# Two-layer graph transformer convolution on Trainium2: another order of the steps in a round

## The chip, the cores and the metric

The kernel runs on one core of one Trainium2 chip. The metric is the time of the program on the device in microseconds (us); lower is better. The kernel before was timed in three runs, with a median of 2658.26 us (2657.74 to 2663.06).

## The reference

The graph has 6250 nodes of 128 features and 106250 edges (self loops among them), sorted by destination. An edge's 96 attributes are 32 cosines of a time difference and 64 given numbers. Two transformer convolutions with two heads run one after the other, with a batch norm and a relu between them; a residual and a layer norm follow.

```python
def _transformer_conv(h, edge_attr, src, dst, Wq, bq, Wk, bk, Wv, bv, We, Ws, bs):
    q, k, v = ...                                   # (n, H, C) each, C = 64
    e = (edge_attr @ We).reshape(-1, H, C)
    kj = k[src] + e
    alpha = jnp.einsum('ehc,ehc->eh', q[dst], kj) / jnp.sqrt(C)
    amax = segment_max(alpha, dst, num_segments=n)
    ex = jnp.exp(alpha - amax[dst])
    den = segment_sum(ex, dst, num_segments=n)
    a = ex / den[dst]
    out = segment_sum((v[src] + e) * a[:, :, None], dst, num_segments=n)
    return out.reshape(n, H * C) + h @ Ws + bs
...
rel_t_enc = jnp.cos((last_update[src] - t)[:, None] * time_w[None, :] + time_b)
edge_attr = jnp.concatenate([rel_t_enc, msg], axis=-1)
h = relu(batch_norm(_transformer_conv(x, edge_attr, src, dst, ...)))
h = _transformer_conv(h, edge_attr, src, dst, ...)
x = layernorm(x + h)
```

## The kernel before

The edges are cut into 104 chunks of 1024 (eight tiles of 128). `conv(c, ...)` runs once for each convolution, c = 0 and c = 1, and its main loop (from L1203) does one round for each chunk. A round k works on several chunks at different stages: it fetches one some rounds ahead, turns k + 1, scores k, sums k − 1, joins k − 2 and finishes k − 3. The order is written out by hand: the loop calls the steps below one after the other, and every engine runs its instructions in the order in which they were called. SP's queue carries most loads and stores, GpSimd's (POOL) the gathers, ScalarE's (ACT) a few others.

The steps, with their lines:

- fetch (from L900): SP loads a chunk's query tables (`ftab`), in c = 1 also its attribute features and residual rows.
- gather (L942): eight indirect transfers on POOL bring the source rows of a chunk into one of seven ring slots (`fring`), a tile each. Through `bring(rows, behind)` a gather can be made to wait for a TensorE step, so that gathers keep TensorE's pace.
- encode (L975 to L988) and sine (L994), c = 0 only: VectorE (DVE) reduces the angles of the cosine, `farg`, and ACT applies the sine. For chunks 43 to 84 encode runs three rounds ahead of the chunk, for the others two; in the former the sine is done for two chunks at once. place (L997) stores the attributes, ea_d.
- feature transposes (`turn_rows`, L1015, tile `fpx`) with ACT's copy to `fft` (L1019), and in c = 0 attribute transposes (`turn_terms`, L1027, `fpe`) with the copy to `fet` (L1028) and a store by SP to et_d. Each of the two is done in two halves of four tiles.
- score (L1058, `fps`): the attention scores. lowest (L1066, L1068): DVE takes their minimum, `fm`. weigh (L1073): ACT's exponential, `fs`.
- weights' transposes (`turn_weights`, L1082, `fppt`) and ACT's copy `fpt` (L1083).
- sums (`gather_sums`, L1105, `fpa`): weighted sums of the gathered rows and attributes. They need fpt.
- divide (L1114 to L1121): DVE divides by the weights' sum (`finv`, `fa`) and makes a selection matrix (`fsel`).
- joins (`finish_turn`, L1136): two transposing matmuls through `fsel` into the same PSUM buffer, and DVE's copy `fat` (L1138).
- product (L1144/1145 in c = 0, L1150/1151 in c = 1): the projection of `fat`, again into that buffer. complete (L1166 in c = 0, from L1173 in c = 1) reads it and adds the skip or residual (`fres`); store (L1183 to L1186) ends c = 1.
- mark (L927 to L930), c = 0: which node of the group an edge belongs to.
- tables: in most rounds one piece of other work is pulled from a list (L635 to L643 the tables of later chunks, `fpg`; L1398 and what follows for the batch norm).

All transposes and tables share four PSUM buffers. The scores have one buffer in c = 0 and two in c = 1. `fpa` has two: the sums of a chunk take the buffer of the chunk two before, once complete has read it.

## Time and profile before

| | |
|---|---|
| median of three runs | 2658.26 us |
| the profiled execution's own time | 2659.45 us |
| its span in the profile | 2657.7 us |
| TensorE (PE) busy | 1857.7 us, 70% |
| GpSimd (POOL) busy | 1583.8 us, 60% |
| VectorE (DVE) busy | 1139.7 us, 43% |
| ScalarE (ACT) busy | 965.5 us, 36% |
| DMA engines busy, mean | queue of SP and ACT loads 36.8%, of the gathers 17.1% |

The profile is of one execution. Its span runs from the first to the last instruction; 1.75 us of the time lie around it. A row of the timeline gives the start, the duration, engine, line and operation, written and read tiles, and in brackets how long the engine stood idle before it and what ended that. "issue" means that the profile shows nothing that the engine waited for, "remote" that the releaser is not known. The ends of matmuls are modelled.

### The profile page before, as it was taken

The page shows a single profiled execution, that of the slowest core. Times are in us where ns is not written, and L with a number is a line of the kernel's source. Part 1 is how long each engine was busy: PE and PEld are TensorE (multiplying, and loading weights), DVE is VectorE, ACT ScalarE, POOL GpSimd, SP SyncE. Part 2 cuts the span into 40 slices and gives each one's busy share as a digit, 9 for nine tenths or more (in the row PEclk, how much of TensorE's full clock was granted, in tenths as well). Part 3 has the DMA queues.
Part 4 walks back from the last instruction along what each step waited for, and adds up shares of the span by engine and source line. Part 5 has one row for each costly group of instructions (what it writes and reads, how often), then busy time and mean ns, then how long its engine had stood idle before and what let it go on. Part 6 is the DMA issues. An engine that isn't in the chain of part 4 may idle for free.

```text
span 2657.7 us, 43186 instructions
## 1 busy us (share of the span) xinstructions
PE 1857.7 (70%) x13293; PEld 1010.6 (38%) x13293; DVE 1139.7 (43%) x3734; ACT 965.5 (36%) x1838; POOL 1583.8 (60%) x1687
## 2 busy tenths in 40 slices
PE   5476776777777777676776676777776776776676
PEld 3243343444333434343443333333333333333333
DVE  4465556556555555465644322332223322232223
ACT  1355545544344343354552222222222222222222
POOL 5256666666666666666626666666666666666663
PEclk9699988989889888889787888888788878788878
DMA  6366665666566665666647555555646555556452
GB/s 181 98 193 181 175 173 158 175 171 176 154 181 175 177 166 158 183 160 177 164 138 211 155 140 149 167 150 149 171 136 171 144 149 158 158 139 171 136 138 69
DMA packets 426919, 423.56 MB, mean 159 GB/s; under 512 B 297362, under 2 KB 344384, under 8 KB 423352
## 3 DMA queue, kind: packets, MB, share of 16 engines
q1 hardware_dynamic: 353174, 273.15, 36.8%
q0 software_dynamic: 53184, 109.31, 17.1%
q10 hardware_dynamic: 20322, 38.24, 4.0%
q8 instruction: 109, 1.79, 0.3%
q14 instruction: 130, 1.06, 0.1%
HBM read 274.63 MB, written 142.54 MB: 157 GB/s over the span
## 4 chain that ended last, share of the span: by engine, by line
PE 56%; issue 23%; another core or an unknown queue 8%; ACT 5%; DVE 4%; DMA 2%; SPq 1%; POOL 1%; ACTq 0%; DVEq 0%; POOLq 0%
PE fps L1058 15%; PE fpa L1105 14%; PE fpx L1015 8%; PE fpg L635 5%; PE fpe L1027 4%; PE fppt L1082 3%; PE fpa L1136 2%; PE fpa L1144 1%; PE fpa L1150 1%; PE fpa L1151 1%; ACT fft L1019 1%; ACT L994 1%; DVE fa L1117 1%; DMA fring<-hn_d,fsrcs 1%
## 5 line engine op out<-in xcount | busy, mean ns | idle before, releaser
L942 POOL DMA_INDIRECT fring<-xv_d,fsrcs x814 | 772.6, 949 | 523.9 <-issue 173.0
L942 POOL DMA_INDIRECT fring<-hn_d,fsrcs x774 | 736.4, 951 | 436.8 <-issue 166.8
L1083 ACT COPY fpt<-fppt 128x384 f32<-128x384 f32 x208 | 100.0, 481 | 1337.5 <-remote 642.4
L1105 PE MATMUL fpa<-fring,fpt 128*32 128x256 f32 (+1 forms) x4128 | 470.1, 504 | 143.2 <-issue 136.7
L1058 PE MATMUL fps<-fft,ftab 128*32 128x384 f32 (+1 forms) x1774 | 330.8, 564 | 46.7 <-issue 27.7
L1105 PEld LDWEIGHTS fpa<-fring,fpt 128*32 128x32 f32 (+1 forms) x4128 | 155.4, 140 | 463.9 <-issue 370.6
L1066 DVE TENSOR_REDUCE flow<-fps 128x1 f32<-128x384 f32 x207 | 115.4, 558 | 499.6 <-PE fpx L1015 288.7
L1015 PE MATMUL fpx<-fident,fring 128*128 128x128 f32 x1664 | 278.8, 295 | 66.4 <-issue 56.2
L1027 PE MATMUL fpe<-fident,fring 128*112 128x128 f32 x832 | 145.4, 302 | 213.1 <-issue 206.0
L1019 ACT COPY fft<-fpx 128x512 f32<-128x512 f32 x402 | 233.3, 581 | 112.5 <-remote 63.2
L1015 PEld LDWEIGHTS fpx<-fident,fring 128*128 128x128 f32 x1664 | 213.9, 153 | 84.3 <-issue 70.5
L1027 PEld LDWEIGHTS fpe<-fident,fring 128*112 128x112 f32 x832 | 101.6, 145 | 237.2 <-issue 229.0
L1058 PE MATMUL fps<-fxT,ftab 112*32 112x384 f32 (+2 forms) x900 | 177.4, 556 | 14.0 <-issue 13.6
L1114 DVE TENSOR_SCALAR finv<-fpa 128x1 f32<-128x1 f32 x206 | 32.7, 159 | 359.4 <-PE fps L1058 88.2
L1136 PE MATMUL fpa<-fsel,fa 128*128 128x128 f32 x404 | 89.6, 304 | 121.1 <-issue 65.1
L1058 PE MATMUL fps<-fet,ftab 112*32 112x384 f32 (+2 forms) x960 | 159.4, 454 | 8.6 <-issue 8.3
L1058 PEld LDWEIGHTS fps<-fft,ftab 128*32 128x32 f32 x1774 | 99.6, 126 | 142.1 <-issue 90.3
L987 DVE SCALAR_TENSOR_TENSOR farg<-fangles,farg 128x256 f32<-128x256 f32 x312 | 132.3, 424 | 10.7
L1186 DVE TENSOR_SCALAR fout<-fres,fmean,fvar 64x128 f32<-64x128 f32 x104 | 38.2, 367 | 221.6 <-ACT fvar L1184 70.3
L1028 ACT COPY fet<-fpe 112x512 f32<-112x512 f32 x207 | 124.3, 601 | 15.7 <-PE fpa L1105 6.7
L1082 PE MATMUL fppt<-fident,fs 128*128 128x128 f32 x626 | 115.3, 287 | 16.3 <-issue 13.9
L1073 ACT ACTIVATE fs<-fps,fm 128x384 f32<-128x384 f32 x207 | 120.7, 583 | 8.8 <-DVE fm L1068 4.3
(282 smaller groups left out, 2461.1 us busy)
## 6 DMA issues: line engine op xcount, KB each, us to landing
ea_d<-fring SPq DMA_DIRECT2D x104, 448.0 KB
et_d<-fet SPq DMA_DIRECT2D x104, 448.0 KB
fring<-ea_d SPq DMA_DIRECT2D x104, 448.0 KB
fxT<-et_d SPq DMA_DIRECT2D x104, 448.0 KB
tab_d<-fo ACTq DMA_DIRECT2D x26, 1024.0 KB
ftab<-tab_d SPq DMA_DIRECT2D x832, 32.0 KB
fring<-in_edge_attr SPq DMA_DIRECT2D x103, 256.0 KB
fring<-xv_d,fsrcs POOLq DMA_INDIRECT x814
```

Of the source, the lines that this page charges most:

```text
L635: pl.step = nc.tensor.matmul(pg, a, fT, start=True, stop=True)
L942: row = nc.gpsimd.indirect_dma_start(out=f[:, t, :D + 1 - c], out_offset=None, in_=(h_d[:N, :] if k < RAW else hn_d) if c else pl.xv_d, in ...
L987: nc.vector.scalar_tensor_tensor(arg, turn, -part, arg, op0=OP.mult, op1=OP.add)
L1015: last = nc.tensor.transpose(px[:, t * P:(t + 1) * P], s.x[:, u * 4 + t, 1 - c:1 - c + D], ident)
L1019: nc.scalar.copy(s.ft[:, u * GE:(u + 1) * GE], px)
L1027: last = nc.tensor.transpose(pe[:EC, t * P:(t + 1) * P], s.e[:, u * 4 + t], ident)
L1028: copy(s.et[:, u * GE:(u + 1) * GE], pe[:EC])
L1058: steps.append(nc.tensor.matmul(s.ps[r, to:to + n], s.tab[:kd, r, i], (ets if i else fts)[:kd, at:at + n], start=i == 0, stop=i == 1 and t ...
L1073: nc.scalar.activation(s.s[:, :s.ps.shape[1]], s.ps, AF.Exp, bias=s.bias, scale=-1.0)
L1082: last = nc.tensor.transpose(pp[:, t * P:(t + 1) * P], s.s[:, t * P:(t + 1) * P], ident)
L1105: steps.append(nc.tensor.matmul(s.pa[g * GH:(g + of) * GH].rearrange("p (a d) -> p a d", a=2), s.pt[:, (g * n + t) * GH:(g * n + t + of) * ...
L1136: step = nc.tensor.transpose(s.po[:, i], s.a[:, r], s.sel[:, 0])
```

## The change

The calls of a round are put in another order, and the gathers wait for other steps. In c = 0 TensorE's order was: score, product, weights' transposes, joins, half of the features, half of the attributes, the other halves, tables, sums. It is now: features of the next chunk, weights' transposes, score, attributes, product, joins, tables, sums. In c = 1 it is the same without the attributes. ACT's copies follow. On VectorE encode now stands behind divide and ahead of lowest, complete and the joins' copy; it stood behind those three. Where one chunk's sine is done alone, it now comes after the joins, or ahead of the next encode.

The eight gathers of a round waited for: the end of the previous sums, half the scores, weights' transposes, joins, first half and second half of the next chunk's transposes, one third and two thirds of the sums. They now wait for: the end of the previous sums, feature transposes, weights' transposes, half the scores, all scores; then in c = 1 joins, one third and two thirds of the sums, in c = 0 attribute transposes, joins, one third of the sums. On SP's queue the store of et_d and the sending of finished rows move with the steps that issue them.

```diff
--- before.py
+++ after.py
@@ -987,6 +987,9 @@
                 nc.vector.scalar_tensor_tensor(arg, turn, -part, arg, op0=OP.mult, op1=OP.add)
             nc.vector.tensor_scalar(arg, arg, -3 * HALF_PI, HALF_PI, op0=OP.max, op1=OP.min)
 
+        def lone():
+            return len(args) == 2 and not SINGLE <= args[1] < LATE
+
         def sine():
             arg, *of = args
             args.clear()
@@ -1226,11 +1229,12 @@
                     bring(range(T))
                 elif not filling:
                     bring(range(1), ended)
-                half, scored = score(k) if on(k) else (None, None)
-                if k >= -1 and not filling:
-                    bring((1,), half)
-                if on(k - 3) and k <= SWITCH:
-                    product(k - 3)
+                step = turn_rows(k + 1, 0) if on(k + 1) else None
+                if filling:
+                    bring(range(5), step)
+                step = turn_rows(k + 1, 1) if on(k + 1) else None
+                if k >= -1:
+                    bring((5,) if filling else (1,), step)
                 step = turn_weights(k - 1) if on(k - 1) else None
                 if k >= -1 and not filling:
                     bring((2,), step)
@@ -1238,39 +1242,45 @@
                     place()
                 if on(k - 2):
                     divide(k - 2)
+                for j in (k + 2, k + 3):
+                    if c == 0 and on(j) and encoded(j) == k:
+                        if lone():
+                            sine()
+                        encode(j)
+                half, scored = score(k) if on(k) else (None, None)
+                if k >= -1 and not filling:
+                    bring((3,), half)
+                    bring((4,), scored)
                 if on(k):
                     lowest(k)
+                    weigh(k)
+                if not c:
+                    send()
+                    step = None
+                    for u in range(2 if on(k + 1) else 0):
+                        step = turn_terms(k + 1, u)
+                    if k >= -1:
+                        bring((5,), step)
+                    send()
                 if on(k - 3) and k <= SWITCH:
+                    product(k - 3)
                     complete(k - 3)
                 elif not c:
                     send()
-                if on(k - 2):
-                    step = finish_turn(k - 2)
+                step = finish_turn(k - 2) if on(k - 2) else None
                 if k >= -1 and not filling:
-                    bring((3,), step)
-                step = turn_in(k + 1, 0) if on(k + 1) else None
-                if k >= -1:
-                    bring(range(5) if filling else (4,), step)
-                if on(k):
-                    weigh(k)
-                step = turn_in(k + 1, 1) if on(k + 1) else None
-                if k >= -1:
-                    bring((5,), step)
-                if not c:
-                    send()
-                for j in (k + 2, k + 3):
-                    if c == 0 and on(j) and encoded(j) == k:
-                        encode(j)
-                        if not SINGLE <= j < LATE:
-                            sine()
+                    if c:
+                        bring((5,), step)
+                    else:
+                        bring((6,), step)
+                if lone() or len(args) == 3:
+                    sine()
                 if k >= 0:
                     at_round[0] = k
                     if c and hidden:
                         hide(4 if k == 0 else 3)
                     else:
                         pull(extra, (3 if k == 3 else 2) if c and k < 6 else 2 if k < 4 or k > 96 else 1)
-                if len(args) == 3:
-                    sine()
                 if on(k - 2) and k >= SWITCH:
                     finish(k - 2)
                 elif not c:
@@ -1283,7 +1293,7 @@
                     store(*done.pop(0))
                 *steps, ended = gather_sums(k - 1) if on(k - 1) else (None, None, None)
                 if k >= -1:
-                    for t, step in zip((6, 7), steps):
+                    for t, step in zip((6, 7) if c else (7,), steps):
                         bring((t,), step)
             last = NC - 1
```

TensorE in c = 0, one round in the middle, from the scores on (`fft` and `fet` are features and attributes of a chunk, `fppt` the weights, `fpx` and `fpe` the transposes). Before:

```order
L1058 MATMUL fps<-fft,ftab 32x384 x2
L1058 MATMUL fps<-fet,ftab 32x384 x2
L1058 MATMUL fps<-fft,ftab 32x384 x2
L1058 MATMUL fps<-fet,ftab 32x384 x2
L1144 MATMUL fpa<-fat,fwv_141 128x128
L1145 MATMUL fpa<-fat,fwe_112 128x128
L1082 MATMUL fppt<-fident,fs 128x128 x3
L1136 MATMUL fpa<-fsel,fa 128x128 x2
L1015 MATMUL fpx<-fident,fring 128x128 x4
L1027 MATMUL fpe<-fident,fring 112x128 x4
L1015 MATMUL fpx<-fident,fring 128x128 x4
L1027 MATMUL fpe<-fident,fring 112x128 x4
```

Now, a round from its first step to the sums that end it (the table, L1408, is pulled in every second of these rounds):

```order
L1018 MATMUL fpx<-fident,fring 128x128 x8
L1085 MATMUL fppt<-fident,fs 128x128 x3
L1061 MATMUL fps<-fft,ftab 32x384 x2
L1061 MATMUL fps<-fet,ftab 32x384 x2
L1061 MATMUL fps<-fft,ftab 32x384 x2
L1061 MATMUL fps<-fet,ftab 32x384 x2
L1030 MATMUL fpe<-fident,fring 112x128 x8
L1147 MATMUL fpa<-fat,fwv_141 128x128
L1148 MATMUL fpa<-fat,fwe_112 128x128
L1139 MATMUL fpa<-fsel,fa 128x128 x2
L1408 MATMUL fpg<-fident,fhT 128x128 x4
L1108 MATMUL fpa<-fring,fpt 64x256 x2
```

The weights' transposes stood between product and joins and now stand ahead of the scores; the product came right after the scores and now has the attribute transposes before it and the joins behind it.

TensorE in c = 1, from the scores to the first of the sums. Before:

```order
L1058 MATMUL fps<-fft,ftab 32x384 x2
L1058 MATMUL fps<-fxT,ftab 32x384 x2
L1058 MATMUL fps<-fft,ftab 32x384 x2
L1058 MATMUL fps<-fxT,ftab 32x384 x2
L1150 MATMUL fpa<-fwv_142,fat 64x64
L1151 MATMUL fpa<-fwe_145,fat 64x64
L1150 MATMUL fpa<-fwv_142,fat 64x64
L1151 MATMUL fpa<-fwe_145,fat 64x64
L1082 MATMUL fppt<-fident,fs 128x128 x3
L1136 MATMUL fpa<-fsel,fa 128x128 x2
L1015 MATMUL fpx<-fident,fring 128x128 x8
L1105 MATMUL fpa<-fring,fpt 64x256 x2
```

Now, from the feature transposes to the first of the sums:

```order
L1018 MATMUL fpx<-fident,fring 128x128 x8
L1085 MATMUL fppt<-fident,fs 128x128 x3
L1061 MATMUL fps<-fft,ftab 32x384 x2
L1061 MATMUL fps<-fxT,ftab 32x384 x2
L1061 MATMUL fps<-fft,ftab 32x384 x2
L1061 MATMUL fps<-fxT,ftab 32x384 x2
L1153 MATMUL fpa<-fwv_142,fat 64x64
L1154 MATMUL fpa<-fwe_145,fat 64x64
L1153 MATMUL fpa<-fwv_142,fat 64x64
L1154 MATMUL fpa<-fwe_145,fat 64x64
L1139 MATMUL fpa<-fsel,fa 128x128 x2
L1108 MATMUL fpa<-fring,fpt 64x256 x2
```

Between product and sums stood weights' transposes, joins and features; now the joins alone stand there.

VectorE in c = 0, from the minimum to the end of the encoding. Before:

```order
L1066 TENSOR_REDUCE flow<-fps 128x1
L1068 TENSOR_SCALAR fm<-flow 128x1
L1166 TENSOR_TENSOR fres<-fpa,fsk 64x64 x2
L1138 COPY fat<-fpa 128x256
L980 TENSOR_TENSOR frel<-fring,few 128x8
L981 TENSOR_TENSOR farg<-frel,fangles 128x256
L982 TENSOR_TENSOR farg<-farg,fangles 128x256
L984 TENSOR_SCALAR fangles<-farg 128x256
L985 TENSOR_SCALAR fangles<-fangles 128x256
L987 SCALAR_TENSOR_TENSOR farg<-fangles,farg 128x256 x3
L988 TENSOR_SCALAR farg<-farg 128x256
```

Now, from the encoding to the joins' copy; divide (L1117 to L1124 now) stands just ahead of it:

```order
L980 TENSOR_TENSOR frel<-fring,few 128x8
L981 TENSOR_TENSOR farg<-frel,fangles 128x256
L982 TENSOR_TENSOR farg<-farg,fangles 128x256
L984 TENSOR_SCALAR fangles<-farg 128x256
L985 TENSOR_SCALAR fangles<-fangles 128x256
L987 SCALAR_TENSOR_TENSOR farg<-fangles,farg 128x256 x3
L988 TENSOR_SCALAR farg<-farg 128x256
L1069 TENSOR_REDUCE flow<-fps 128x1
L1071 TENSOR_SCALAR fm<-flow 128x1
L1169 TENSOR_TENSOR fres<-fpa,fsk 64x64 x2
L1141 COPY fat<-fpa 128x256
```

The seven steps of encode have moved ahead of the minimum, of complete (`fres`) and of `fat`.

## Rows read from the trace of the kernel before

**Rows 1.** busy us of PE, PEld, DVE, ACT, POOL; clock, DMA, GB/s by stretches
```profile
600.00:680.00 80.00, 58.24 (x434) 33.58 (x433) 47.98 (x152) 37.15 (x59) 49.67 (x53) 0.91 0.66 179
2200.00:2280.00 80.00, 54.88 (x391) 28.12 (x387) 21.14 (x79) 19.10 (x50) 49.13 (x52) 0.85 0.55 154
2620.00:2645.00 25.00, 23.12 (x231) 12.15 (x231) 11.37 (x48) 11.10 (x34) 3.01 (x4) 0.90 0.08 18
```

**Rows 2.** timeline of POOL, second convolution: start, us, instruction [idle, releaser]
```profile
1909.00 0.95 POOL L942 DMA_INDIRECT fring<-hn_d,fsrcs  x1 [1.57 <-PE fps L1058]
...
1912.76 0.95 POOL L942 DMA_INDIRECT fring<-hn_d,fsrcs  x1 [0.30 <-issue]
1915.30 0.95 POOL L942 DMA_INDIRECT fring<-hn_d,fsrcs  x1 [1.59 <-remote]
...
1922.95 0.95 POOL L942 DMA_INDIRECT fring<-hn_d,fsrcs  x1 [1.69 <-PE fpa L1151]
```

**Rows 3.** timeline of PE, the same round of the second convolution
```profile
1909.32 0.55 PE L1082 MATMUL fppt<-fident,fs 128*128 128x128 f32 x3
1910.06 0.44 PE L1136 MATMUL fpa<-fsel,fa 128*128 128x128 f32 x2 [0.19 <-DVE fsel L1121]
1910.33 1.04 PE L1015 MATMUL fpx<-fident,fring 128*128 128x128 f32 x8
1911.21 1.02 PE L635 MATMUL fpg<-fhT,fm 128*128 128x512 f32 x2
1915.98 2.99 PE L1105 MATMUL fpa<-fring,fpt 128*64 128x256 f32 x20 [3.75 <-issue]
1918.74 1.51 PE L1058 MATMUL fps<-fft,ftab 128*32 128x384 f32 x8
...
1921.46 0.48 PE L1150 MATMUL fpa<-fwv,fat 128*64 128x64 f32 x2
...
1922.12 0.28 PE L1151 MATMUL fpa<-fwe,fat 128*64 128x64 f32 x2
1922.69 0.55 PE L1082 MATMUL fppt<-fident,fs 128*128 128x128 f32 x3 [0.28 <-PE fpa L1151]
```

**Rows 4.** timeline of ACT, then of DVE, the same round
```profile
1915.07 0.48 ACT L1083 COPY fpt<-fppt 128x384 f32<-128x384 f32 x1 [8.97 <-remote]
...
1914.92 0.56 DVE L1066 TENSOR_REDUCE flow<-fps 128x1 f32<-128x384 f32 x1 [4.92 <-remote]
...
1915.59 0.28 DVE L1173 SCALAR_TENSOR_TENSOR fres<-fpa,fr 64x128 f32<-64x128 f32 x1
```

**Rows 5.** timeline of PE, a round of the first convolution
```profile
612.77 1.65 PE L1105 MATMUL fpa<-fring,fpt 128*64 128x256 f32 x20
614.24 0.38 PE L1058 MATMUL fps<-fft,ftab 128*32 128x128 f32 x2
...
617.81 0.49 PE L1144 MATMUL fpa<-fat,fwv 128*128 128x128 f32 x2
...
618.36 0.49 PE L1082 MATMUL fppt<-fident,fs 128*128 128x128 f32 x3
```

**Rows 6.** timeline of ACT, the end of that round
```profile
622.98 0.48 ACT L1083 COPY fpt<-fppt 128x384 f32<-128x384 f32 x1 [5.93 <-remote]
```

**Rows 7.** timeline of ACT, after the last gather
```profile
2632.45 0.48 ACT L1083 COPY fpt<-fppt 128x384 f32<-128x384 f32 x1 [1.81 <-PE fppt L1082]
```

**Rows 8.** groups of the page: xcount | busy, mean ns | idle before
```profile
L942 POOL DMA_INDIRECT fring<-xv_d,fsrcs x814 | 772.6, 949 | 523.9 <-issue 173.0
L942 POOL DMA_INDIRECT fring<-hn_d,fsrcs x774 | 736.4, 951 | 436.8 <-issue 166.8
```

**Rows 9.** timeline of DVE, the same round of the first convolution: encoding's ends
```profile
611.97 0.18 DVE L980 TENSOR_TENSOR frel<-fring,few 128x8 f32<-128x8 f32 x1
...
615.40 0.29 DVE L988 TENSOR_SCALAR farg<-farg 128x256 f32<-128x256 f32 x1
```

## The prediction

> **What bounds the kernel now.** I read busy times by stretches first, then one round of the timeline, engine by engine. No engine is full: of 80 us in the first convolution TensorE is busy for 58.24 and GpSimd for 49.67 [rows 1]. In two stretches of 80 us, one in each convolution, GpSimd ran 53 and 52 gathers [rows 1]. A round of the main loop issues eight, so a round takes 80 / 53 × 8 = 12.1 and 80 / 52 × 8 = 12.3 us; I reckon with 12.3 in both. In the last stretch, with four gathers left, TensorE is busy for 23.12 of 25 us, against 54.88 to 58.24 of 80 before [rows 1]. So TensorE's work does not fill a round while gathers run. What does?
>
> GpSimd first. From 1909.00 to 1912.76 there are three steps of 1.25 us: 0.95 for a gather and 0.30 between two. Then it stands for 1.59 us in place of 0.30, runs five, and stands for 1.69 [rows 2]. Eight gathers without a stop are 8 × 1.25 = 10.0 us; the round has 12.3, and a stop costs about 1.3 beyond the normal gap, so there are (12.3 − 10.0) / 1.3 = 1.8 stops in a round.
>
> TensorE next. The weights' transposes end at 1909.32 + 0.55 = 1909.87, yet ScalarE's copy of them, fpt, starts at 1915.07 [rows 3, 4]: 5.20 us. TensorE has joins, feature transposes and tables to do, then stands for 3.75 us until the sums at 1915.98. The first gather after GpSimd's stop starts at 1915.30 [rows 2], beside it. In the earlier convolution the same copy starts at 622.98, after transposes that ended at 618.36 + 0.49 = 618.85: 4.13 us [rows 5, 6]. After the last gather the copy at 2632.45 is released by its own transposes, which the earlier one, released by "remote", is not [rows 4, 7]. I read this as: while gathers run, a TensorE result reaches ScalarE and VectorE late, in bursts around GpSimd's stops. Call it the **lag**. A round is a loop that holds one lag. In the round shown: sums to score 2.76, score to product 2.72, product 0.94, a gap of 0.29, weights 0.55, lag 5.20, copy and hand-over 0.91. That is 13.37 us, exactly the distance between the two weights' transposes, 1909.32 and 1922.69 (the product ends at 1922.12 + 0.28) [rows 3].
>
> **The change, part by part.** No matmul, transpose, copy or transfer is added or removed; everything is order and what the gathers wait for.
>
> *Weights' transposes early.* Score, product and joins (in the first convolution the attribute transposes too) now lie between them and the sums that need fpt. With the pieces above that is 2.72 + 0.94 + 0.44 + 1.02 for tables = 5.1 us of TensorE work as cover, against 2.5 (joins, rows, tables) before. A lag of 4.1 to 5.2 is then almost covered, and the 3.75 us of idle ahead of the sums would fall to nothing if nothing else were late.
>
> *Joins after the product.* They need divide, which needs the sums' signal. Between sums and joins there were score, product and weights; now there are rows as well. Divide starts earliest at the lag's end and the joins were short by 0.19 [rows 3], so this costs nothing and gains at most that.
>
> *What is late next: the product.* The sums write one of two PSUM buffers (fpa). The one they need still belongs to the chunk two ahead, until complete has read its product. Already now the sums at 1915.98 start just behind that read (fres, 1915.59 + 0.28 = 1915.87) [rows 3, 4]. Before, weights, joins, rows and tables stood between product and sums; now only joins and tables do, 1.4 us. The new loop in the second convolution is: sums 2.76, rows 0.88, weights 0.55, score 2.72, product 0.94, lag, then lowest and complete 1.06 (1914.92 to 1915.98): 8.91 + lag. It takes 12.3 us at a lag of 3.4. In the first convolution: sums 1.47, rows 1.04, weights 0.49, score 3.57, attribute transposes 1.04, product 0.55 [rows 5] (1.04 is for eight [rows 3]), and about 1.2 for lowest and complete: 9.4 + lag, 12.3 us at a lag of 2.9.
>
> *How long this lag is* no row shows. From below it is nothing, as after the last gather [rows 7]; from above 5.20. I take it by the gathers' new waits: gather 5 of the second convolution now waits for the joins, just behind the product, so a stop falls there. Joins 0.44 and a stop of 1.6 make 2.0. The loop is then 10.9, under what GpSimd needs with one stop, 10.0 + 1.3 = 11.3. So I take 11.3 there: 1.0 us less in each of 774 / 8 = 97 rounds [rows 8], **−97 us**. In the first convolution gather 5 waits for the attribute transposes, ahead of the product, and gather 6 for the joins. One more gather lies between, 1.25 + 1.6 = 2.9, and the loop is back at 12.3: **nothing** for 814 / 8 = 102 rounds.
>
> *Encoding ahead of the minimum.* It takes 3.7 us of VectorE (611.97 to 615.69) and used to stand ahead of the next round's divide [rows 9]. Now lowest and complete queue behind it. After the sums: a lag of 2.0, divide 1.1, encoding 3.7, lowest and complete 1.2 make 8.0, with the sums 9.5; the round has 12.3, so it is covered, by 2.8 us. For chunks 43 to 84 it is done three chunks ahead, and its last gather was issued only in the round before; a landing later than those 2.8 us holds lowest and complete and so the sums. From below it gains nothing more than the above; from above I give it 42 × 2.5 = +105 us, about half of the encoding and its landing. I take nothing, since the first convolution is held at 12.3 anyhow.
>
> *ScalarE's order, SP's stores.* The copies go the way of their transposes and ScalarE is idle for 8.97 us ahead of fpt [rows 4]. The et_d store moves with the attribute copies, some 2 us later in the round; it is read only in the second convolution. Both nothing.
>
> **The sum** goes against the profiled run's own 2659.45 us (span 2657.7): 2659.45 − 97 = 2562. The median of the runs is 1.2 lower, so I give 2561.
>
> [...] No row shows transposes to have lowered the clock, so it has 0.03, within the second rival.
>
> **The rivals.**
> 1. *The product's lag stays long, and it is slower.* Place: the sums' PSUM buffer, with rows, weights and attribute transposes now inside the loop. With the shortest lag seen for fpt, 4.13, the loops are 13.0 and 13.5: +0.7 × 97 + 1.2 × 102 = +190, 2849. It decides from a lag of 3.4 (second) and 2.9 (first convolution); with the first alone it is 2780, and a little past the point 2690. For it: the lags of fpt are all above that point. Against: they ended at stops, and the stops now fall elsewhere. 0.30.
> 2. *One stop in both convolutions.* The first gains 1.0 too: 2659 − 1.0 × 199 = 2460. For it: fpt's cover, the earlier divide. Against: the longer loop. 0.20.
> 3. *Nothing.* GpSimd's two stops stay, only waiting for other steps; the round is 12.3 as now: 2658. For it: stops are ended by gathers whose TensorE step was long done (1915.30, "remote"). 0.10.
>
> **How the numbers follow.** My forecast, one stop in the second convolution alone, has 0.40: 2561, with 2500 to 2640 its own range. Faster by over 0.2% (5.3 us, about what a measurement here can tell): 0.40 + 0.20 = 0.60; within: 0.10; slower: 0.30. The range is 2430 to 2740: the low end takes in 2460 and a bit more, the high end rival 1 where the lag lies just past its point; left out are the long lags (0.13) and under one stop (0.06). Without any stop it would be 2659 − 2.3 × 199 = 2201, which I don't expect in any case.
>
> **What would show it.** Right: in the second convolution 80 us hold 56 to 57 gathers in place of 52 (8 × 80 / 11.3), one gap over 1 us per eight gathers, idle ahead of the sums under 1.5 us and ended by fres, fpt's copy off the waits' top. Wrong: complete's read of the product (fres) starts 4 us or more behind the product, with the sums right behind it, and 49 gathers or fewer in 80 us; or 52 to 53 as now. If VectorE waits ahead of the encoding's first operation (frel) in the first convolution, the encoding's place has cost what I put at nothing.

## The result and the profile after

The changed kernel takes 2693.29 us (median of 5 runs, 2684.68 to 2700.10); the kernel before took 2660.55 beside it (5 runs). The ratio is 1.0124, with a 95% interval of 1.0100 to 1.0148. It is 1.2% slower, where 2561 was forecast. Below, a point is 0.01 of such a ratio. The profiled execution took 2684.68 us, its span is 2682.9 us at a mean granted clock of 0.817 (before 0.853).

Busy time by stretches of the changed kernel (stretch, length, then PE, PEld, DVE, ACT and POOL with counts, clock, DMA share, GB/s):

```profile
600.00:680.00 80.00, 58.85 (x438) 34.83 (x439) 46.46 (x147) 35.41 (x57) 49.16 (x53) 0.81 0.63 175
2200.00:2280.00 80.00, 50.91 (x382) 26.78 (x382) 22.31 (x82) 21.61 (x55) 47.72 (x52) 0.79 0.49 139
```

GpSimd again runs 53 and 52 gathers in these stretches, as in [rows 1]. The saved stop is not there. Where do the 25 us of span come from? The minima of the scores, one for each chunk, are numbered through both convolutions (0 to 103 and 104 to 207). Their starts in the two timelines tell it:

| chunk's minimum | before, us | after, us | difference |
|---|---|---|---|
| first of the first convolution (0) | 117.1 | 120.6 | +3.5 |
| number 95 | 1273.7 | 1274.7 | +1.0 |
| number 103, last of the first convolution | 1352.0 | 1358.6 | +6.7 |
| number 108 | 1454.4 | 1465.0 | +10.6 |
| number 204 | 2617.4 | 2644.2 | +26.8 |

The steady rounds of the first convolution cost what they did. Its last rounds, which have no gathers beside them, and the start of the second convolution cost 10 us of the difference; the 96 rounds from 108 to 204 cost 16, or 0.17 us each.

The same stretch of the second convolution as in [rows 3], TensorE:

```profile
1907.58 2.65 PE L1108 MATMUL fpa<-fring,fpt 128*64 128x256 f32 x20 [3.35 <-issue]
1910.15 1.67 PE L1018 MATMUL fpx<-fident,fring 128*128 128x128 f32 x8
1911.66 0.49 PE L1085 MATMUL fppt<-fident,fs 128*128 128x128 f32 x3
1912.08 0.87 PE L1061 MATMUL fps<-fft,ftab 128*32 128x384 f32 x8
...
1913.93 0.28 PE L1154 MATMUL fpa<-fwe,fat 128*64 128x64 f32 x2
1914.15 0.44 PE L1139 MATMUL fpa<-fsel,fa 128*128 128x128 f32 x2
1914.42 1.02 PE L635 MATMUL fpg<-fhT,fm 128*128 128x512 f32 x2
1919.38 2.99 PE L1108 MATMUL fpa<-fring,fpt 128*64 128x256 f32 x20 [3.93 <-issue]
```

ScalarE and VectorE in that round:

```profile
1912.79 0.50 ACT L1086 COPY fpt<-fppt 128x384 f32<-128x384 f32 x1
...
1916.12 0.56 DVE L1069 TENSOR_REDUCE flow<-fps 128x1 f32<-128x384 f32 x1 [3.35 <-PE fpg L635]
...
1918.98 0.28 DVE L1176 SCALAR_TENSOR_TENSOR fres<-fpa,fr 64x128 f32<-64x128 f32 x1 [2.11 <-remote]
```

and GpSimd (three of the nine gathers from 1911.78 to 1923.58):

```profile
1911.78 0.94 POOL L942 DMA_INDIRECT fring<-hn_d,fsrcs  x1 [1.94 <-PE fpx L1018]
...
1920.53 0.95 POOL L942 DMA_INDIRECT fring<-hn_d,fsrcs  x1 [0.30 <-issue]
1923.58 0.94 POOL L942 DMA_INDIRECT fring<-hn_d,fsrcs  x1 [2.10 <-PE fpx L1018]
```

The weights' transposes are now copied to fpt at 1912.79, 0.64 us behind their end at 1911.66 + 0.49 = 1912.15, where it was 5.20 us in [rows 3, 4]. In their place the sums wait for 3.93 us for something else. The product ends at 1913.93 + 0.28 = 1914.21; complete reads it (fres) at 1918.98, 4.77 us later; that read is over at 1919.26 and the sums start at 1919.38. The profile calls this wait "issue"; that it is the wait for fres is read from the times. It is so throughout: from chunk 5 to 100 and from 108 to 204 the sums start 0.11 to 0.17 us behind the end of complete's read in all 191 rounds. Before the change they did so, within 0.25 us, in 25. GpSimd has one stop in this round, but of 1.94 and 2.10 us, not 1.6. From 1500 to 2550 us it has 156 gaps of over 1 us among 684 gathers, 1.8 in eight.

In the first convolution the release is seen by name. TensorE (product, sums), then VectorE (encoding's end, minimum, complete):

```profile
620.89 0.39 PE L1148 MATMUL fpa<-fat,fwe 128*128 128x128 f32 x2
...
626.61 1.71 PE L1108 MATMUL fpa<-fring,fpt 128*64 128x256 f32 x8 [4.25 <-DVE fres L1169]
...
624.16 0.29 DVE L988 TENSOR_SCALAR farg<-farg 128x256 f32<-128x256 f32 x1
625.34 0.56 DVE L1069 TENSOR_REDUCE flow<-fps 128x1 f32<-128x384 f32 x1 [0.89 <-remote]
...
626.01 0.46 DVE L1169 TENSOR_TENSOR fres<-fpa,fsk 64x64 f32<-64x64 f32 x2
```

The product ends at 620.89 + 0.39 = 621.28; fres starts at 626.01; the sums stand idle for 4.25 us and are released by it. But the 4.73 us between are not all the product's: the encoding occupies VectorE until 624.45, the minimum starts 0.89 us later, and complete, which stands behind both, follows it directly. So 4.73 is the most that this lag can be. In the second convolution's round complete stood idle for 2.11 us of its own. Counted over chunks 12 to 94 and 110 to 200, VectorE stood over 0.3 us idle right ahead of complete in 20 of 82 rounds of the first convolution and in 36 of 90 of the second; in the others complete started straight behind other work of VectorE, the minimum as a rule, so what came last there was the scores' result or the encoding.

The longest waits in all (engine, line waited at, releaser: us in total, times, longest), after:

```profile
PE fpa L1108 <- issue: 439.9, 107, 8.2
...
DVE flow L1069 <- remote: 384.2, 93, 8.2
...
PE fpa L1108 <- DVE fres L1169: 131.6, 44, 6.3
```

and before, the groups whose place they took:

```profile
ACT fpt L1083 <- remote: 642.4, 92, 15.2
ACT fpt L1083 <- PE fpx L1015: 552.3, 85, 11.3
...
PE fpa L1105 <- issue: 136.7, 66, 4.6
```

ScalarE's wait for the weights' transposes, 642 + 552 us, is gone; it had not been a loss in itself, since ScalarE has time: after the change it is busy for 985.8 us, 37% of the span. What counts is TensorE's idle time ahead of the sums: 137 us before, 440 + 132 us after under the two largest releasers.

### The profile page after: what moved, and what is told of

Read it like the earlier page. It is cut to its first block, busy times and chain, and to the rows that moved or that the text cites. A ratio compares the mean times of both kernels' runs of the same rounds, so it can differ in the third digit from the quotient of the medians.

```text
span 2682.9 us, 42690 instructions
## 1 busy us (share of the span) xinstructions
PE 1799.9 (67%) x13293; PEld 1024.9 (38%) x13293; DVE 1146.5 (43%) x3734; ACT 985.8 (37%) x1836; POOL 1580.1 (59%) x1687
## 3 DMA queue, kind: packets, MB, share of 16 engines
q14 instruction: 130, 1.06, 0.1%
## 4 chain that ended last, share of the span: by engine, by line
PE 53%; issue 22%; DVE 8%; another core or an unknown queue 8%; DMA 3%; ACT 2%; POOL 2%; DVEq 0%; SPq 0%; ACTq 0%; POOLq 0%
PE fpa L1108 18%; PE fps L1061 11%; PE fpx L1018 10%; PE fppt L1085 3%; PE fpg L635 2%; POOL fring L942 2%; PE fpe L1030 2%; PE fpa L1139 2%; DMA fring<-xv_d,fsrcs 2%; DVE farg L987 2%; DVE flow L1069 1%; PE fpa L1153 1%; ACT fs L1076 1%; PE fpa L1154 1%
## 5 line engine op out<-in xcount | busy, mean ns | idle before, releaser
L1108 PE MATMUL fpa<-fring,fpt 128*32 128x256 f32 (+1 forms) x4128 | 527.0, 561 | 729.1 <-issue 439.9
L1108 PEld LDWEIGHTS fpa<-fring,fpt 128*32 128x32 f32 (+1 forms) x4128 | 169.7, 149 | 1031.8 <-issue 980.6
L1018 PE MATMUL fpx<-fident,fring 128*128 128x128 f32 x1664 | 333.2, 364 | 29.9 <-issue 10.2
L1018 PEld LDWEIGHTS fpx<-fident,fring 128*128 128x128 f32 x1664 | 266.2, 191 | 179.6 <-issue 155.8
L1061 PE MATMUL fps<-fft,ftab 128*32 128x384 f32 (+1 forms) x1774 | 258.6, 496 | 2.9 <-issue 2.8
L1117 DVE TENSOR_SCALAR finv<-fpa 128x1 f32<-128x1 f32 x206 | 33.1, 161 | 418.0 <-PE fppt L1085 127.3
L1061 PE MATMUL fps<-fet,ftab 112*32 112x384 f32 (+2 forms) x960 | 137.0, 447 | 0.2 <-issue 0.2
L1085 PE MATMUL fppt<-fident,fs 128*128 128x128 f32 x626 | 130.7, 329 | 6.9 <-DVE fhn L1411 6.0
L1061 PE MATMUL fps<-fxT,ftab 112*32 112x384 f32 (+2 forms) x900 | 122.9, 472 | 4.2 <-issue 4.2
L1030 PE MATMUL fpe<-fident,fring 128*112 128x128 f32 x832 | 116.4, 282 | 8.5 <-issue 4.8
L1085 PEld LDWEIGHTS fppt<-fident,fs 128*128 128x128 f32 x626 | 100.5, 179 | 11.2 <-issue 9.5
```

Of the source, the lines that this page charges most:

```text
L1018: last = nc.tensor.transpose(px[:, t * P:(t + 1) * P], s.x[:, u * 4 + t, 1 - c:1 - c + D], ident)
L1030: last = nc.tensor.transpose(pe[:EC, t * P:(t + 1) * P], s.e[:, u * 4 + t], ident)
L1061: steps.append(nc.tensor.matmul(s.ps[r, to:to + n], s.tab[:kd, r, i], (ets if i else fts)[:kd, at:at + n], start=i == 0, stop=i == 1 and t ...
L1085: last = nc.tensor.transpose(pp[:, t * P:(t + 1) * P], s.s[:, t * P:(t + 1) * P], ident)
L1108: steps.append(nc.tensor.matmul(s.pa[g * GH:(g + of) * GH].rearrange("p (a d) -> p a d", a=2), s.pt[:, (g * n + t) * GH:(g * n + t + of) * ...
```

## The experiments

The main theory after the result was the prediction's first rival. **Theory A**: the sums wait for the PSUM buffer that complete frees, since the product now stands late in the round and its result is known late. **Theory B**: gathers on GpSimd make TensorE's results late and set a round of some 12.1 us whatever the order. **Theory C**: the encoding ahead of the minimum costs. **Theory D**: each step that TensorE must signal for a gather alone delays the others.

The runs fell into two kinds, which was not expected. In three sets of runs the kernel before took 2626.88, 2655.72 and 2660.49 us; in two it took 2158.15 and 2158.03. Each ratio below is to the kernel before in the same set. The first kind is called "late", the second "prompt", for a reason shown below. The expectations call them two kinds of chips. That is not shown: the record has chip number 9 both for the late set with 2660.49 us and for the prompt one with 2158.03, some 18 minutes later. The unaltered change was not run in a prompt set.

**The change once more** (late). 

> The changed kernel, unaltered, as the measure for the three beside it. On a chip where the kernel before takes some 2630 to 2660 us (TensorE's results late while gathers run): a ratio of 1.010 to 1.015, as first measured. On a chip like that of the last four runs, where it takes 2158 and results are known at once: 1.015 to 1.03, with the loss in the first convolution.

Measured: 1.0129 (1.0099 to 1.0158). As forecast: the loss repeats.

**A third buffer for the sums** (late).

```diff
-p_tr = ... tile_pool(name=f"fp_tr{c}", bufs=4, ...)
+p_tr = ... tile_pool(name=f"fp_tr{c}", bufs=3, ...)
-p_a = ... tile_pool(name=f"fp_a{c}", bufs=2, ...)
+p_a = ... tile_pool(name=f"fp_a{c}", bufs=3, ...)
```

> The changed kernel with three PSUM buffers for the sums (fpa) in place of two, and three for the transposes in place of four; nothing else. Theory A (the sums wait for complete of the chunk that holds their buffer, because its product's result is known late): that chunk is now one older, the wait of the sums for fres goes, and the time falls below the kernel before, to 2560 to 2640. Theory B (GpSimd's gathers and the lateness of all TensorE results set the round, whichever wait ends last): another result is late in its place, 2670 to 2710. Theory C (the encoding ahead of the minimum costs): 2670 to 2700, since VectorE's order is as it was.

Measured: 1.0034 (1.0021 to 1.0047). Its waits ahead of the sums:

```profile
PE fpa L1108 <- issue: 142.4, 222, 3.8
```

and no row for fres among the longest. So the wait for the buffer was there, and this exchange of buffers takes about 0.9 of the 1.25 points off. But the time did not fall below the kernel before, as A had forecast, so A is not all.

The same two lines changed in the kernel before (late). 

> The kernel before with three buffers for the sums and three for the transposes. Theory A says that the old order doesn't wait for the buffer alone (fpt comes as late): 0.995 to 1.005 where results are late. If the buffer bounds the old order as well: 0.98 to 0.993, and the new order costs nothing of its own. With one transpose buffer fewer hurting: over 1.005.

Measured: 1.0077 (1.0060 to 1.0094), the branch "one transpose buffer fewer hurting". The same exchange that takes 0.9 points off the new order adds 0.8 to the old one. A wait shows that is not among those of the kernel before, feature transposes that wait for a copy out of a transpose buffer:

```profile
PE fpx L1015 <- ACT fpt L1083: 62.9, 26, 5.5
```

So the old order gains nothing from the exchange, as A says. What the third buffer is worth without the lost one is not separated, in either order.

**The product ahead of the weights' transposes** (late).

```diff
+                if on(k - 3) and k <= SWITCH:
+                    product(k - 3)
                 step = turn_weights(k - 1) if on(k - 1) else None
...
                 if on(k - 3) and k <= SWITCH:
-                    product(k - 3)
                     complete(k - 3)
```

> The changed kernel with the product moved ahead, between the feature transposes and the weights' transposes; two buffers as before. Theory A: weights, score, (attributes), joins and tables then lie between product and sums, so fres is early; 2560 to 2650. Theory B: 2670 to 2710, with the sums' idle time as long and another releaser. Theory C: no change from 2693.

Measured: 1.0051 (1.0034 to 1.0069): 0.7 points less than the change and again not below the kernel before. It does not bear A out as put, for fres did not become early. Product, minimum, complete and sums of one round:

```profile
1908.32 0.28 PE L1154 MATMUL fpa<-fwe,fat 128*64 128x64 f32 x2
...
1916.05 0.56 DVE L1069 TENSOR_REDUCE flow<-fps 128x1 f32<-128x384 f32 x1 [4.74 <-remote]
...
1916.72 0.27 DVE L1176 SCALAR_TENSOR_TENSOR fres<-fpa,fr 64x128 f32<-64x128 f32 x1
...
1917.10 2.54 PE L1108 MATMUL fpa<-fring,fpt 128*64 128x256 f32 x20 [4.36 <-issue]
```

The product ends at 1908.60, but its reader stands behind the minimum on VectorE, and the minimum waits for the scores. The sums still start directly behind fres, in 190 of 191 rounds. The edit moved the product and left complete where it was.

**The encoding back behind the joins' copy** (late, twice).

```diff
-                for j in (k + 2, k + 3):
-                    if c == 0 and on(j) and encoded(j) == k:
-                        if lone():
-                            sine()
-                        encode(j)
                 half, scored = score(k) if on(k) else (None, None)
...
                 step = finish_turn(k - 2) if on(k - 2) else None
...
+                for j in (k + 2, k + 3):
+                    if c == 0 and on(j) and encoded(j) == k:
+                        encode(j)
+                        if not SINGLE <= j < LATE:
+                            sine()
```

> The changed kernel with the encoding (and its sine) at its old place, behind complete and the joins' copy. Theory C: the first convolution gets faster by 0.2 us a round or more, 2640 to 2675. Theory A: the first convolution took as long as before the change already, so within 10 us of 2693; if the minimum and complete come earlier for it, some 20 us less at most. Theory B: the same, 2685 to 2700.

> The changed kernel with the encoding at its old place, once more. Where results are late: as the unaltered change, within 0.003 (1.0127 was measured). Where they are not late, theory C (the encoding, waiting for its chunk's last gather, holds the minimum and complete): the rounds of chunks 43 to 84 fall from 10.8 to 10.0 us and the ratio to 1.000 to 1.008; theory A: within 0.004 of the unaltered change.

Measured: 1.0127 (1.0106 to 1.0148), and 1.0102 (1.0079 to 1.0125) beside the change's 1.0129. The first had no unaltered change beside it and is like the change's 1.0124 and 1.0129; in the second the encoding's place is worth about 0.3 points, with intervals that overlap. So C falls as the main cause where results are late. Where they are prompt it was not tried.

A part of the loss is the encoding's all the same, in the rounds without gathers at the end of the first convolution. In the change's trace (scores, then encoding's first and last step, minimum):

```profile
1338.24 0.84 PE L1061 MATMUL fps<-fet,ftab 112*32 112x384 f32 x8
...
1339.30 0.17 DVE L980 TENSOR_TENSOR frel<-fring,few 128x8 f32<-128x8 f32 x1 [1.88 <-DMA fring<-xv_d]
...
1342.80 0.29 DVE L988 TENSOR_SCALAR farg<-farg 128x256 f32<-128x256 f32 x1
1343.00 0.55 DVE L1069 TENSOR_REDUCE flow<-fps 128x1 f32<-128x384 f32 x1
```

The scores end at 1339.08. The encoding waits for its chunk's rows and then runs, and the minimum follows it, 3.92 us behind the scores. From the minimum of chunk 100 to that of chunk 103 the change took 25.3 and 23.0 us in its two traces, with the encoding back 20.1 in both, the kernel before 19.8.

**Fewer gather waits.** Gathers wait no more for half the scores, nor for a third and two thirds of the sums.

```diff
-                    bring((3,), half)
-                    bring((4,), scored)
+                    bring((3, 4), scored)
...
-                    if c:
-                        bring((5,), step)
-                    else:
-                        bring((6,), step)
+                    bring((5, 6, 7) if c else (6, 7), step)
...
-                if k >= -1:
-                    for t, step in zip((6, 7) if c else (7,), steps):
-                        bring((t,), step)
+                if filling:
+                    bring((6, 7))
```

The first run was prompt. 

> The changed kernel with fewer gather waits: none on half the scores, nor on a third and two thirds of the sums. Gathers 3 and 4 wait for all scores, the last two or three for the joins (their last wait stays on a step whose result VectorE or ScalarE needs anyway). TensorE then has three signals fewer in a round. Theory D (while gathers run, TensorE's signals go out one by one, some 2 us apart, and each signal kept for a gather alone delays those behind it): a ratio of 0.95 to 0.99 to the kernel before. Theory B (the gathers with their stops bound the round, however they are paced): 1.00 to 1.02. Theory A (the sums' buffer alone): 1.012, as the change.

Measured: 1.0235 (1.0218 to 1.0252), outside all three ranges. Late: 

> The changed kernel with three gather waits fewer, once more, because the last four runs fell on a chip without late results and so could not tell. Where results are late, theory D (signals go out one by one beside the gathers): at least 0.02 below the unaltered change in ratio, 0.95 to 0.99. Theory B: within 0.004 of the unaltered change. Where they are not late: 1.02 to 1.03, as before.

Measured: 1.0018 (1.0008 to 1.0027), 1.1 points less than the change beside it, between the two ranges. The sums still start directly behind fres, in 189 of 191 rounds. In the kernel before, first prompt: 

> The kernel before with the same taken away: gather 1 waits for all scores in place of half, gathers 6 and 7 for nothing of their own. Theory D: as much is gained as in the changed kernel, a ratio of 0.95 to 0.99. Theory B: 0.99 to 1.01. That the gathers' pace protects the loads beside them (why it is there) would show as slower, 1.01 to 1.03.

Measured: 1.0001 (0.9992 to 1.0011). Late: 

> The kernel before with three gather waits fewer, once more. Where results are late, theory D: 0.95 to 0.985; theory B: 0.995 to 1.005. Where they are not late: 1.000, as before.

Measured: 0.9984 (0.9971 to 0.9996). So D, as put, falls: three steps fewer to signal gave 1.1 points in the new order and 0.16 in the old, not 2 to 5 in both. What the new order loses to these waits is shown; whether to the waiting of GpSimd or to the signals is not.

**Buffer or early product with fewer waits**, to see whether the costs add. The first run was prompt. 

> The changed kernel with both: a third buffer for the sums and the three gather waits taken away. Theories A and D together: the lowest of these, a ratio of 0.94 to 0.985 to the kernel before. Theory B: 1.00, as with the buffer alone.

Measured: 1.0261 (1.0241 to 1.0280), outside both ranges. Late, this one and the next: 

> The changed kernel with the third buffer for the sums and three gather waits fewer, once more, because the first run of it fell on a chip without late results. Where results are late: if the two costs are apart, each takes its own part (0.9 and 1.1 points) off 1.0125 and the ratio is 0.990 to 0.996, below the kernel before; if both only bring the sums' start to the same next limit, 1.000 to 1.004.

Measured: 1.0017 (1.0005 to 1.0030).

> The changed kernel with the product ahead of the weights' transposes and three gather waits fewer. If the place of the product and the gather waits are the change's two costs: 0.990 to 0.998 where results are late. If the product's place is no cost once the waits are gone: as with fewer waits alone, 1.000 to 1.004.

Measured: 1.0011 (1.0000 to 1.0021). Both pairs are where one common limit was forecast: the costs don't add. Each of the three edits brings the new order back to about the old order's time, and neither of the two pairs that were run goes below it. That fits theory B. What sets the limit these runs do not show; with fewer waits the sums still wait for fres, only for less long.

A rival was not tried. The granted clock goes with the time: in the late sets the new order as it is, with the encoding back, and the old order with buffers exchanged (1.0077 and more) were granted 0.812 to 0.827, the new order with the other edits (1.0051 and less) 0.830 to 0.872, the kernel before 0.840 to 0.860. Whether a lower clock made the rounds longer or longer waits lowered the clock, no run separates.

**The gathers taken away**, so that B's cause can be seen. All of them (late):

```diff
-                row = nc.gpsimd.indirect_dma_start(out=f[:, t, :D + 1 - c], ..., in_offset=...)
+                row = nc.sync.dma_start(f[:, t, :D + 1 - c], table[t * P:(t + 1) * P, :])
```

> The changed kernel with each gather on GpSimd replaced by a copy of 128 fixed rows of the same size, issued by SP; the rows' indices are left out, so the gathered features are not those of the edges. Theory B: TensorE's results are then known at once, as they are after the last gather, and a round takes the 6 to 9 us of those last rounds: 1700 to 2200 in all. Theory A alone (the lateness is not from GpSimd): the sums still wait for fres, 2500 to 2700.

Measured: 0.9000 (0.8976 to 0.9024). TensorE's feature and weights' transposes and ScalarE's copy of the latter:

```profile
1914.33 0.48 PE L1017 MATMUL fpx<-fident,fring 128*128 128x128 f32 x1 [0.62 <-DMA fring<-hn_d]
1914.60 0.85 PE L1084 MATMUL fppt<-fident,fs 128*128 128x128 f32 x3
...
1915.48 0.48 ACT L1085 COPY fpt<-fppt 128x384 f32<-128x384 f32 x1
```

The copy starts 0.03 us behind the transposes (1914.60 + 0.85 = 1915.45): nothing is late here. The round is 11.24 us here (the weights' transposes stand at 1903.36 and at 1914.60), not 6 to 9, because the copies now come late from SP's queue: the feature transposes wait for them (0.62 us in the row), and in the first convolution so does the encoding, which holds complete and the sums. In all, the encoding waits 253.3 us for its copies there, and the sums 305.9 us for fres. So the size missed, for new waits that the experiment made itself. Half of them, every second gather, first prompt. 

> The changed kernel with every second gather replaced by a copy of 128 fixed rows from SP; the indices of those are left out, so half of the gathered features are not those of the edges. Theory D: GpSimd gathers for 5 us of a round, the signals are late only beside them, and the round falls at least half of the way to that with plain copies alone (a ratio of 0.90): 0.90 to 0.95. That lateness depends on the transfers in flight rather than on GpSimd's work: no change from the changed kernel, 1.00 to 1.015.

Measured: 0.9600 (0.9560 to 0.9640), a smaller gain than D's. Late: 

> The changed kernel with every second gather replaced by a copy of 128 fixed rows from SP (their indices left out), once more. Where results are late: if the lateness comes from GpSimd's gathers, it falls with their number, a ratio of 0.90 to 0.96; if it comes from the transfers in flight, whose number is the same, 1.00 to 1.02.

Measured: 0.7947 (0.7933 to 0.7962), a median of 2116.67 us; the way that was forecast for lateness from the gathers, and far beyond its range. Its second convolution:

```profile
1900.00:1980.00 80.00, 63.30 (x563) 35.36 (x561) 30.33 (x114) 29.15 (x75) 36.14 (x38) 0.90 0.80 210
```

38 gathers in 80 us, at four a round, are a round of 80 / 38 × 4 = 8.4 us. TensorE's weights' transposes and product, ScalarE's copy, complete's read:

```profile
1907.54 0.49 PE L1089 MATMUL fppt<-fident,fs 128*128 128x128 f32 x3
...
1909.81 0.28 PE L1158 MATMUL fpa<-fwe,fat 128*64 128x64 f32 x2
...
1909.19 0.50 ACT L1090 COPY fpt<-fppt 128x384 f32<-128x384 f32 x1
...
1912.14 0.28 DVE L1180 SCALAR_TENSOR_TENSOR fres<-fpa,fr 64x128 f32<-64x128 f32 x1
```

The weights' transposes end at 1908.03 and fpt follows at 1909.19, behind the feature copies; the product ends at 1910.09 and its read is at 1912.14, 2.05 us later, in place of 4.77. The bytes moved are the same (423.5 MB); half of GpSimd's gathers are gone. So in the late sets the lateness comes with the gathers on GpSimd and falls with their number; the new order then runs a round of this stretch in 8.4 us. Whether it is GpSimd's work or the transfers of its own queue is not separated, for both are halved together, and the copies' rows lie side by side where a gather's lie apart.

**Gaps between gathers** (both prompt): a fill of an unused tile behind the fourth and eighth gather, with fewer waits, in the new and in the old order.

```diff
+                if t in (3, 7):
+                    nc.gpsimd.memset(idle, 0.0)
```

> The changed kernel with three gather waits fewer, and behind the fourth and the eighth gather of a round a fill of an unused tile on GpSimd (about half a microsecond), so that it leaves gaps without waiting for TensorE. If a gap of some 0.9 us between two gathers lets TensorE's results out, a round needs 8 x 1.25 + 2 x 0.6 = 11.2 us of GpSimd and its stops for TensorE go: where results are late, a ratio of 0.92 to 0.97. If a fill does not serve as a gap, or the stops stay beside it: 1.00 to 1.04. Where results are not late (kernel before at 2158): GpSimd bounds the round, 1.08 to 1.12.

> The kernel before with three gather waits fewer and the same two fills. Where results are late, if gaps let them out: 0.92 to 0.97; otherwise 1.00 to 1.04. Where they are not late: 1.08 to 1.12.

Measured: 1.0969 (1.0951 to 1.0988) and 1.0851 (1.0832 to 1.0869), both within the range given for prompt results. Against the same two kernels without the fills in the other prompt set (2208.54 and 2159.27 us) that is 160 and 183 us, or 0.81 and 0.92 us more in each of 199 rounds. A fill of 128x464 took 0.485 us on GpSimd in the kernel before, so two are about 1.0 us: from this the author's estimate is that GpSimd's added work sets the round. In a prompt row (below) fpt is 0.03 us behind its transposes, which leaves no lateness to take away, so whether gaps help where results are late stays open.

**What prompt runs show.** Stretches of the kernel before with fewer waits, both convolutions:

```profile
600.00:680.00 80.00, 65.22 (x514) 42.07 (x514) 51.88 (x169) 42.71 (x68) 60.49 (x65) 0.87 0.76 208
...
1800.00:1880.00 80.00, 60.93 (x506) 32.29 (x506) 27.29 (x101) 26.76 (x70) 60.51 (x65) 0.84 0.64 177
```

65 gathers in 80 us are a round of 9.85 us, close to the 1.25 × 8 = 10.0 that GpSimd needs without a stop. Weights' transposes and their copy:

```profile
1601.27 0.55 PE L1082 MATMUL fppt<-fident,fs 128*128 128x128 f32 x3
...
1601.85 0.48 ACT L1083 COPY fpt<-fppt 128x384 f32<-128x384 f32 x1 [2.46 <-PE fppt L1082]
```

The copy starts 0.03 us behind the transposes' end (1601.82), with gathers running. The new order with the same few waits:

```profile
600.00:680.00 80.00, 61.83 (x501) 37.52 (x502) 50.69 (x160) 40.43 (x67) 57.29 (x61) 0.90 0.76 204
...
1800.00:1880.00 80.00, 62.82 (x482) 32.15 (x483) 27.03 (x99) 26.11 (x65) 60.49 (x65) 0.85 0.69 188
```

It has GpSimd's pace in the second convolution, and only 61 gathers in 80 us in the first. Its waits name two reasons, complete's read and the encoding's wait for its chunk's gather:

```profile
PE fpa L1108 <- DVE fres L1169: 234.1, 87, 11.8
...
DVE frel L980 <- DMA fring<-xv_d,fsrcs: 123.2, 39, 7.1
```

Which of the two costs the 1.0235 there was not separated by a run of its own. The third buffer gave nothing (1.0261), though with it the sums no longer start behind fres; VectorE's wait ahead of the encoding stays (162.7 us). The loss lies in the first convolution: from chunk 0 to 95 the new order takes 975.7 us and the old one, with the same few waits, 927.9. That points to the encoding's place.

## Why the prediction was wrong

- *"While gathers run, a TensorE result reaches ScalarE and VectorE late"*: right for late runs, and now shown by taking gathers away. That it comes "in bursts around GpSimd's stops" was too simple: fres at 1918.98 lies within a run of eight gathers without a stop, at the end of the sixth.
- *Weights' transposes early*: right. fpt came 0.64 us behind them, and the sums' wait for it went.
- *What is late next, the product*: right in place. The sums start directly behind fres, in both convolutions and in every round. That only the product's own result makes fres late is not so: complete stands behind the minimum and in the first convolution behind the encoding too.
- *"How long this lag is"*: here it failed. I took 2.0 us because a gather now waits for the joins and a stop would fall there. The round shown has 4.77 us in the second convolution (1914.21 to 1918.98), and at most 4.73 in the first (621.28 to 626.01), the length that fpt's lag had. Over the 90 and 82 rounds counted above, the medians from the product's end to fres are 4.6 and 3.7 us; the unaltered change's second trace has 4.4 and 3.7. Rival 1 said that it decides from 3.4 us in the second convolution. No row showed the new order's lag, but the kernel before has rows of the old order's, which were not read:

```profile
1909.10 0.28 PE L1151 MATMUL fpa<-fwe,fat 128*64 128x64 f32 x2
...
618.13 0.39 PE L1145 MATMUL fpa<-fat,fwe 128*128 128x128 f32 x2
...
622.87 0.46 DVE L1166 TENSOR_TENSOR fres<-fpa,fsk 64x64 f32<-64x64 f32 x2 [0.71 <-remote]
```

From the product's end to fres they take 6.21 us in the second convolution (1909.38 to 1915.59 [rows 4]) and 4.35 in the first (618.52 to 622.87), the latter with VectorE idle right ahead of fres. With a lag of this size the prediction's own loops come out slower than 12.3.

- *"1.0 us less in each of 97 rounds, −97 us"*: in its place 0.17 us more a round, and 10 us at the turn between the convolutions, for which the sum had no term. There no gathers run, and from the minimum of chunk 100 to that of chunk 103 it now takes 25.3 us (1333.4 to 1358.6), where it took 19.8 (1332.2 to 1352.0). Nearly all of these 5.5 us go when the encoding goes back (20.1); what makes the rest of the turn longer is open.
- *Rival 1's price*, 2849, was far too high, though its sign held. I took the loop's pieces from one round with a slow TensorE (its mean granted clock from 1915.9 to 1922.7 was 0.55): 7.85 us from the sums' start to the product's end. After the change they take 6.63 (1907.58 to 1914.21), with a hand-over of 0.40 in place of 1.06. 6.63 + 4.77 + 0.40 = 11.80, the distance of the sums at 1907.58 and 1919.38. Also, "the lags of fpt are all above that point" held for the two rounds read, not for all: in 20 of 82 rounds of the first convolution it is under 2.9, the point there.
- *First convolution: nothing*: right in size for the steady rounds (3.5 us late at chunk 0, 1.0 at chunk 95), and partly by luck. The reason given was a lag of 2.9 in a loop of 9.4 + lag; the median is 3.7, and the other pieces came out shorter.
- *Encoding: nothing*: right within 0.3 points where results are late, but not at its ends. The sign named for it came: VectorE stood 59.9 us ahead of frel in all, before 8.0. In steady late rounds that is hidden; in the last rounds of the first convolution it is not (see above).
- *GpSimd's floor*: 10.0 us a round is real (9.85 in prompt runs), but my 11.3 with one stop was not reached over the stretch, which has 52 gathers as before, with 1.8 stops in eight gathers.
- *Transposes and the clock*: the 0.03 was for a clock that gains when the run of transposes is parted by the scores and the product. No run shows such a gain as the transposes' own: with them parted the granted clock fell from 0.853 to 0.817, with the third buffer besides it was 0.859 to 0.872, and no run here separates what moved it.

## What to carry to other kernels

When a step is moved, look at what it frees as well as at what it needs: here the product's reader frees one of two PSUM buffers, and moving the product late put other steps and a late result into the loop that the sums wait for. Ask where the reader stands in its own engine's order too: moving the product back alone left complete behind the minimum. A long wait that disappears is worth nothing when the next one ends at the same time (ScalarE's 642 + 552 us went, and the kernel got 1.2% slower); ask for the next releaser and give it the lateness that the trace shows, not one that the plan would like. Waits put in only to pace a queue belong to the order they were made for: the three taken away cost the new order 1.1 points and the old one 0.16.

## What was not expected of the hardware

- The kernel before takes 2158 us in some sets of runs and 2627 to 2660 in others, with the same program. In the former (with fewer waits), fpt follows its transposes by 0.03 us in the row shown, with gathers running; in the latter by a median of 4.0 us in the first convolution and 4.5 in the second. Whether this belongs to the chip or changes with time, and why, is open.
- Where results were late, half of the gathers on GpSimd replaced by copies of the same size took the changed kernel from a ratio of 1.013 to 0.795; where they were prompt the same kernel has 0.960. The two absolute times are close, 2117 and 2072 us.
